# One wait for the four gathers of a half, and the item-0 corrections moved behind the spike counts, in a recurrent spiking recommender on one core

## The chip, the cores and the metric

The kernel runs on one core of a Trainium2 chip. The metric is the time of one execution in microseconds (us) on the device. The prediction was made on 1649.73 us, the median of three runs of the kernel before (1649.36 to 1651.72). All runs of this study were on single cores, but not all on the same chip. That turned out to matter, so each result below says which chip it comes from, by its number. The first pair of measurements, on which the prediction is judged, came without a chip number.

## The reference, cut to what matters

```python
e = emb[seq]                                  # 1024 sequences, 50 items each, rows of 128 floats
prefix = jnp.cumsum(e, axis=1)
denom = jnp.minimum(t_idx[None, :], lengths[:, None])
uF = prefix / denom[:, :, None]
y = (uF - uF.mean(axis=0)) * lax.rsqrt(uF.var(axis=0) + 1e-5) * gamma + beta
# per time step: v += (x - v) / 2; spike = v >= 1; v -= spike
uF_out = spikes.mean(axis=0)
scores = uF_out @ emb.T                       # 1024 x 100001
```

Row 0 of the table counts as zero. The kernel gathers the row as it is and takes it out again with a small matmul; this is the "correction".

## The kernel before

There are two stages. The first goes through the 50 time steps, the second multiplies the spike means by the whole table and stores 409.6 MB of scores. The change is in the first. In each step GpSimd gathers the rows of the next step with eight indirect transfers of 128 rows each. TensorE transposes the eight tiles of this step into two accumulators (`pre[0]`, `pre[1]`, one for each half of the batch). VectorE reads each half (`uF`), takes its statistics, and updates the membrane `v`.

```python
gp = ph.enter_context(tc.tile_pool(name="gather", bufs=2))     # two buffers of e
...
        def gather(t):
            es[t] = gp.tile([P, B], F32, tag="e", name=f"e_{t}")
            for n in range(NB):                                # NB = 8
                nc.gpsimd.indirect_dma_start(
                    out=es[t][:, n * P : (n + 1) * P], out_offset=None, in_=table,
                    in_offset=bass.IndirectOffsetOnAxis(ap=idx[:, n, t : t + 1].bitcast(U32), axis=0),
                )
...
            if t + 1 < T:
                gather(t + 1)
            e = es.pop(t)
            ...
            for h, cs in enumerate(halves):
                for k in range(0, BANK, P):                    # four transposes for each half
                    nc.tensor.matmul(pre[h][:, k : k + P],
                                     lhsT=e[:, h * BANK + k : h * BANK + k + P], rhs=ident,
                                     start=False, stop=last, is_transpose=True, ...)
                nc.vector.scalar_tensor_tensor(uF[:, cs], rlen[:, cs], 1.0 / (t + 1), pre[h], ALU.max, ALU.mult)
                nc.vector.bn_stats(bs[:, h, :], uF[:, cs])
            if not last:
                correct(t + 1, l)                              # two matmuls into pre[0], pre[1]
            ...
            if t and not last:
                nc.vector.tensor_single_scalar(s, v, V_TH, ALU.is_ge)
                counted(t - 1, s)                              # two matmuls into sums[0], sums[1]
            # ... normalisation and the step of v on VectorE and ScalarE
```

## Time and profile before

| | kernel before, first measurement |
|---|---|
| time | 1649.73 us |
| profiled span | 1646.4 us |
| last `uF` of stage 1 starts | 576.37 us |
| last gather starts | 567.84 us |
| a step that nothing holds up | 7.49 us |
| three steps, on average | 33.9 us |
| GpSimd waits "remote" for its buffer | 64.2 us in 16 waits |

In a line of the timeline the first number is the start in us and the second the duration, then come the engine, the line of the source, the operation, output <- inputs, the shape and the number of instructions. The bracket is the idle time of the engine just before, and what ended it. "Remote" means that no instruction in the profile ended just then: what ended the wait was done earlier, and I take it that its semaphore came late: in the stall that the prediction shows, the eight transposes had all started by 308.70 us and were recorded as reported up to 321.10 us. The lines of before that matter stand in the prediction.

### The profile page before, as it was taken

The page shows a single profiled execution, that of the slowest core. Times are in us where ns is not written, and L with a number is a line of the kernel's source. Part 1 is how long each engine was busy: PE and PEld are TensorE (multiplying, and loading weights), DVE is VectorE, ACT ScalarE, POOL GpSimd, SP SyncE. Part 2 cuts the span into 40 slices and gives each one's busy share as a digit, 9 for nine tenths or more (in the row PEclk, how much of TensorE's full clock was granted, in tenths as well). Part 3 has the DMA queues.
Part 4 walks back from the last instruction along what each step waited for, and adds up shares of the span by engine and source line. Part 5 has one row for each costly group of instructions (what it writes and reads, how often), then busy time and mean ns, then how long its engine had stood idle before and what let it go on. Part 6 is the DMA issues. An engine that isn't in the chain of part 4 may idle for free.

```text
span 1646.4 us, 12555 instructions
## 1 busy us (share of the span) xinstructions
PE 1115.2 (68%) x4538; PEld 829.4 (50%) x4548; DVE 940.4 (57%) x1161; ACT 630.6 (38%) x700; POOL 379.3 (23%) x406
## 2 busy tenths in 40 slices
PE   4344433444334498889987888888888888788885
PEld 2122211222113276667766666666666666666664
DVE  4566655666556766557655555555555555555553
ACT  2222222222222255446544444444444444444442
POOL 7666666666666500000000000000000000000000
PEclk9999999999755599999999999999999999999998
DMA  9511111111111179999999999999999999999898
GB/s 342 213 45 48 47 48 43 47 48 48 48 43 49 39 320 412 416 422 398 426 422 429 432 428 427 421 420 429 420 423 412 415 421 421 428 425 423 381 428 350
DMA packets 53691, 488.14 MB, mean 296 GB/s; under 512 B 11995, under 2 KB 12796, under 8 KB 32380
## 3 DMA queue, kind: packets, MB, share of 16 engines
q1 hardware_dynamic: 31984, 428.77, 62.0%
q0 software_dynamic: 12800, 26.24, 5.5%
q10 hardware_dynamic: 8844, 32.33, 5.0%
q8 instruction: 36, 0.59, 0.1%
q14 instruction: 27, 0.22, 0.0%
HBM read 77.69 MB, written 409.60 MB: 296 GB/s over the span
## 4 chain that ended last, share of the span: by engine, by line
DMA 48%; DVE 22%; another core or an unknown queue 10%; PE 9%; ACT 5%; issue 4%; POOL 1%; DVEq 0%; ACTq 0%; SPq 0%
DMA scores<-o 48%; PE po L149 8%; ACT o L456 4%; DVE bs L306 4%; DVE uF L305 4%; DVE v L342 3%; DVE s L326 3%; DVE negv L348 3%; DVE o L454 2%; POOL e L187 1%; DVE a L335 1%; DVE mv L316 1%; DVE q L332 0%; PE pt L119 0%
## 5 line engine op out<-in xcount | busy, mean ns | idle before, releaser
L454 DVE TENSOR_SCALAR o<-po 128x1024 f32<-128x1024 f32 x391 | 463.7, 1221 | 352.4 <-DMA scores<-o 326.9
L456 ACT ACTIVATE o<-po 128x1024 f32<-128x1024 f32 (+1 forms) x391 | 388.0, 1019 | 548.2 <-DMA scores<-o 345.0
L187 POOL DMA_INDIRECT e<-in_L_rec_emb_table,idx x400 | 378.6, 947 | 188.8 <-issue 109.8
L149 PE MATMUL po<-pairs,countB 128*128 128x512 f32 x1168 | 313.9, 415 | 66.8 <-ACT o L456 49.6
L149 PEld LDWEIGHTS po<-pairs,countB 128*128 128x128 f32 x1168 | 225.4, 198 | 131.3 <-ACT o L456 64.4
L149 PE MATMUL po<-pairs,countC 128*128 128x512 f32 x876 | 238.2, 417 | 43.2 <-ACT o L456 43.0
L253 PE MATMUL pre<-zT,l 128*128 128x512 f32 x100 | 74.6, 748 | 247.2 <-DVE uF L305 159.5
L149 PEld LDWEIGHTS po<-pairs,countC 128*128 128x128 f32 x876 | 168.8, 199 | 89.3 <-ACT o L456 54.8
L253 PEld LDWEIGHTS pre<-zT,l 128*128 128x128 f32 x100 | 27.7, 279 | 286.9 <-issue 183.0
L305 DVE SCALAR_TENSOR_TENSOR uF<-rlen,pre 128x512 f32<-128x512 f32 x100 | 68.0, 680 | 180.5 <-remote 145.0
L320 ACT ACTIVATE r<-mv,eps 128x1 f32<-128x1 f32 x50 | 14.7, 295 | 378.8 <-DVE mv L316 269.4
L142 DVE TENSOR_TENSOR pairs<-pt,pairs 128x1024 fp32r<-128x1024 f32 (+1 forms) x73 | 88.4, 1217 | 94.7 <-ACT pairs L141 94.7
L296 PE MATMUL pre<-ident,e 128*128 128x128 f32 x400 | 107.2, 426 | 25.8 <-DMA e<-in_L_rec_emb_table,idx 17.7
L119 PE MATMUL pt<-ident,rows 128*128 128x128 f32 x782 | 113.1, 292 | 8.3 <-ACT o L456 3.7
L119 PEld LDWEIGHTS pt<-ident,rows 128*128 128x128 f32 x782 | 102.3, 154 | 28.6 <-issue 9.8
L296 PEld LDWEIGHTS pre<-ident,e 128*128 128x128 f32 x400 | 85.3, 223 | 60.9 <-DMA e<-in_L_rec_emb_table,idx 32.2
L149 PE MATMUL po<-hi,countB 128*128 128x512 f32 x200 | 82.9, 414 | 19.2 <-ACT o L456 14.9
L264 PE MATMUL sums<-s,ident_h 128*128 128x512 bf16 x88 | 45.3, 606 | 64.2 <-DVE s L326 32.8
L149 PE MATMUL po<-lo,countB 128*128 128x512 f32 x200 | 80.4, 402 | 0.0
L149 PE MATMUL po<-pairs,countA 128*128 128x512 f32 (+1 forms) x292 | 73.5, 393 | 9.1 <-ACT o L456 9.1
L141 ACT CAST pairs<-pt 128x1024 fp32r<-128x1024 f32 (+1 forms) x73 | 73.6, 1008 | 15.0 <-PE pt L119 14.9
L149 PE MATMUL po<-hi,countC 128*128 128x512 f32 x150 | 63.2, 421 | 17.7 <-ACT o L456 17.7
(76 smaller groups left out, 849.8 us busy)
## 6 DMA issues: line engine op xcount, KB each, us to landing
scores<-o SPq DMA_DIRECT2D x96, 3072.0 KB, 20.3
scores<-o SPq DMA_DIRECT2D x32, 1536.0 KB, 9.0
rows<-in_L_rec_emb_table ACTq DMA_DIRECT2D x20, 1536.0 KB, 29.2
scores<-o SPq DMA_DIRECT2D x22, 1024.0 KB, 8.6
rows<-in_L_rec_emb_table SPq DMA_DIRECT2D x6, 3072.0 KB, 42.7
scores<-o SPq DMA_DIRECT2D x8, 2048.0 KB, 13.2
scores<-o SPq DMA_DIRECT2D x8, 1872.5 KB, 11.3
e<-in_L_rec_emb_table,idx POOLq DMA_INDIRECT x400
```

What stands on the lines that cost most here:

```text
L119: nc.tensor.transpose(pt[:, k0 : k0 + kw], r[:kw, k0 : k0 + D], ident[:kw, :kw])
L141: nc.scalar.copy(vh, vp)
L142: nc.vector.tensor_tensor(vl, vp, vh.bitcast(F32), ALU.subtract)
L149: nc.tensor.matmul(po[:, :kw], lhsT=counts[n], rhs=part[:, k0 : k0 + kw], start=j == 0, stop=j == 1,)
L187: nc.gpsimd.indirect_dma_start(out=es[t][:, n * P : (n + 1) * P], out_offset=None, in_=table, in_offset=bass.IndirectOffsetOnAxis(ap=idx[: ...
L253: nc.tensor.matmul(pre[h], lhsT=l, rhs=zT[:, h * BANK : (h + 1) * BANK], start=t == 0, stop=False, skip_group_check=True,)
L296: nc.tensor.matmul(pre[h][:, k : k + P], lhsT=e[:, h * BANK + k : h * BANK + k + P], rhs=ident, start=False, stop=last, is_transpose=True, ...
L305: nc.vector.scalar_tensor_tensor(uF[:, cs], rlen[:, cs], 1.0 / (t + 1), pre[h], ALU.max, ALU.mult)
L306: nc.vector.bn_stats(bs[:, h, :], uF[:, cs])
L326: nc.vector.tensor_single_scalar(s, v, V_TH, ALU.is_ge)
L454: nc.vector.tensor_scalar_mul(o[:, h0 : h0 + hw], po[:, :hw], 1.0 / T)
L456: nc.scalar.mul(o[:, h0 : h0 + hw], po[:, :hw], 1.0 / T)
```

## The change

It is meant to spare waits and semaphore updates on TensorE's queue: the first transpose of a half waits for all four of its gathers, so that the other three need no wait and their increments can be merged; and the corrections come behind the counts, so that they need no wait for VectorE.

```diff
+    def after(ins, other):
+        sync = mybir.DependencyInfo(mybir.DependencyClass.Sync, mybir.DependencyReason.DATA)
+        tc.add_manual_dep(ins.ins, other.ins.name, sync, reason="one wait for several gathers")
...
-                nc.gpsimd.indirect_dma_start(
+                landed[t, n] = nc.gpsimd.indirect_dma_start(
...
-                    nc.tensor.matmul(
+                    turn = nc.tensor.matmul(
...
+                    if k == 0 and not last:
+                        for n in range(1, BANK // P):
+                            after(turn, landed[t, h * BANK // P + n])
...
-            if not last:
-                correct(t + 1, l)
-            else:
+            if last:
...
                 counted(t - 1, s)
+            if not last:
+                correct(t + 1, l)
```

More of the change, by code (lines that the diff above doesn't have):

```diff
@@ L182, in rec_kernel @@
         es = {}
+        landed = {}
         def gather(t):
```

## The prediction

> **What bounds the kernel now.** I read the page first, then the chain of waits in order of time, then the timeline of a few steps of the first stage, and last the semaphore records behind it. The row of slices shows two stages: about 576 us of 50 time steps (GpSimd gathers, DMA almost idle at 45 to 50 GB/s), then 1070 us in which output stores run at some 415 GB/s. The change touches the first stage only, and nothing the second stage waits for except its start: the six big row loads it needs are done in the second of the forty slices. So a microsecond taken from the first stage should be a microsecond of the whole.
>
> ```profile
> POOL 7666666666666500000000000000000000000000
> ...
> DMA  9511111111111179999999999999999999999898
> ...
> L187 POOL DMA_INDIRECT e<-in_L_rec_emb_table,idx x400 | 378.6, 947 | 188.8 <-issue 109.8
> ...
> L305 DVE SCALAR_TENSOR_TENSOR uF<-rlen,pre 128x512 f32<-128x512 f32 x100 | 68.0, 680 | 180.5 <-remote 145.0
> ```
>
> The gathers follow each other every 1.25 us when nothing holds them (947 ns and 0.30 us of issue), so eight cost 10.02 us a step. One undisturbed step takes 7.49 us, and VectorE is busy throughout (7.02 us of records in the 7.48 us from 298.31). Neither explains the stage: v of successive steps starts at 292.25, 299.74, 307.23 and then 326.16 us. Three steps take 33.9 us, 11.3 us each, over the gathers' 10.02. The timeline shows the long one:
>
> ```profile
> 305.79 1.48 PE L296 MATMUL pre<-ident,e 128*128 128x128 f32 x6
> ...
> 307.23 1.23 DVE L342 SCALAR_TENSOR_TENSOR v<-negv,v 128x1024 f32<-128x1024 f32 x1 [0.21 <-DVE negv L348]
> ...
> 307.43 0.47 PE L296 MATMUL pre<-ident,e 128*128 128x128 f32 x1 [0.15 <-issue]
> ...
> 308.70 0.47 PE L296 MATMUL pre<-ident,e 128*128 128x128 f32 x1 [0.80 <-DMA e<-in_L_rec_emb_table,idx]
> ...
> 315.51 0.69 DVE L305 SCALAR_TENSOR_TENSOR uF<-rlen,pre 128x512 f32<-128x512 f32 x1 [7.05 <-remote]
> ...
> 321.12 0.69 DVE L305 SCALAR_TENSOR_TENSOR uF<-rlen,pre 128x512 f32<-128x512 f32 x1 [4.20 <-remote]
> 321.35 0.94 POOL L187 DMA_INDIRECT e<-in_L_rec_emb_table,idx  x1 [4.19 <-remote]
> ```
>
> All eight transposes of the step have started by 308.70 us, the eighth 2.49 us after its gather was issued, so the data is there. Yet uF of the first half, which needs four of them, starts at 315.51, and of the second half at 321.12, 12.4 us after the eighth transpose started. VectorE waits only for TensorE there, so "remote" must be TensorE's completion semaphore arriving late. GpSimd waits for the same eight completions, because e has two buffers, and stands still for 4.19 us. This happens every third step:
>
> ```profile
> DVE uF L305 <- remote: 145.0, 27, 12.4
> ...
> POOL e L187 <- remote: 64.2, 16, 4.4
> ```
>
> The semaphore records say how it is late. Counted back from the two releases, transposes 1 to 5 are reported at 307.78, 310.58, 312.69, 315.48 and 318.28 us, one per 2.1 to 2.8 us; the rest follow quickly (320.38, 320.41, 321.10) once the gathers have stopped at 317.17. In the first step after a stall the reports come at once, 0.21 us apart (291.47, 291.68, 291.89, 292.11). So each report is a queued event that costs 2 to 3 us in the bad stretch. I do not know what makes it slow; it begins after some 11 to 19 us of unbroken gathering and ends when gathering pauses.
>
> [...]
>
> **The change, part by part.** The built programs show what the source does not say.
> 1. Transposes. Before, each of the eight waits for its own gather and raises the semaphore by one. After, the first of a half carries four waits and the other three none, and the increments are merged into one +4 on the fourth. Over the kernel, updates on the transposes fall from 400 to 106. The price is two EventSemaphore instructions per half, 196 in all, 51 ns each in the trace: 0.2 us a step on a queue that is mostly idle.
> 2. Corrections behind the counts. They then need only ScalarE's l, since the counts already waited for a later VectorE instruction. Of 49 EventSemaphore waits one remains, and the updates on corrections and counts fall from 85 + 48 to 45 + 2. A typical step falls from 11 events (8 + 2 + 1) to 3.
> 3. Added latency. The first half's transposes now start only when its fourth gather has landed; four spaced 0.21 us then run where one ran, so each half is ready about 0.65 us later. That shifts every step once and does not lengthen the period. The corrections delay the next transposes by two matmuls: 0.57 + 0.43 us by their spacing at the start of the trace (11.52, 12.09, 12.52). In the undisturbed step the fourth would end near 300.4 instead of 299.4 us and VectorE asks for it at 300.88; the eighth near 301.2, asked for at 302.21. It just fits, at no cost.
> 4. Unchanged: gathers, VectorE and ScalarE work, buffers, the second stage.
>
> What this buys: if the last completion of a step comes less than 8.8 us after its last gather has landed, GpSimd never waits (it asks for the buffer 11.27 us after that gather started, less 2.5 to land). Before it came about 12.4 us late in each stall. With three events, even at 2.8 us each, two of them after the data is there, I estimate 1.1 us + 2 x 2.8 = 6.7 us. GpSimd then runs through: from 3.89 us, 399 intervals of 1.2525 us and the first one's extra 0.2 put the last gather at 503.9 instead of 567.84 us. That is 64 us, the same as its waits in the table above. The two steps that also prepare rows (t = 42 and 44) cost VectorE and TensorE some 5 us each; the 2.5 us a step by which VectorE is quicker than the gathers makes that up by t = 49. The last uF then stands near 508 to 511 instead of 576.4. Full gain: 64 + about 1 = 65 us, to 1585 us.
>
> **The rivals.**
> - The slow reports stay and become the new chain. With gathering unbroken the bad stretch may never end. From one second-half uF to the next the path would be counts and corrections (about 5 us), then three reports of 2.1 to 2.8 us: 11.3 to 13.4 us, over 10.02, until GpSimd stalls again and clears it. For it: the cause of the slowness is not removed. Against: one step in three is slow at worst now with 11 events, and GpSimd has 8 us of slack to eat first. It would give back 15 to 45 us: 1600 to 1630.
> - The inserted waits are the poison. TensorE now sits in EventSemaphore instructions for the gathers of every half while a report is pending, and all data must be there before any transpose. For it: stalls mostly begin where TensorE waits for a gather. Against: at t = 0 and 1 it waited for nearly every gather, and reports came 0.5 us after the transposes; in the stall at 547.92 us no transpose waited. It would be 1650 to 1700.
> - VectorE becomes the bound. At 7.49 us a step it would need 375 us, under the gathers' 501, so only if the added microsecond on TensorE opens a bubble over 2.5 us a step; I see none.
> - The second stage starts earlier into something unready. Its rows are loaded long before; nothing speaks for it.
>
> **Range and chances.** I give some 60% to the full gain (1580 to 1592), 22% to a part of it (1600 to 1630), 12% to about no change and 6% to worse. 2% is 33 us, half of the full gain, so most partial gains count as faster too. I put the time at 1590 us, a little above the full gain, and 1577 to 1635 as the range.
>
> **What would show it.** Right: gathers 1.25 us apart from start to end with GpSimd's "remote" wait near zero instead of 64.2 us; the last gather near 504 us; steps of 10.0 us; the second stage as long as before (1070 us). Step 2 is right if uF starts within 1 to 7 us of its fourth and eighth transpose. Wrong: a "remote" wait of VectorE still over 8 us after the eighth transpose, gathers pausing every few steps, or steps over 11 us; then the number of reports was not what mattered.

## The result

The changed kernel took 1653.82 us (1653.41 to 1654.22, 4 runs), the kernel before 1649.55 us beside it (1647.12 to 1651.72, 4 runs). The ratio is 1.0026, with a 95% interval of 1.0009 to 1.0044: the same within 2%. All ratios here are the mean time of one kernel's fast runs over that of the other's of the same rounds, so they are not quite the ratio of the medians.

First the page of the changed kernel, in the lines that answer to those of before (the busy tenths of GpSimd and DMA in forty slices, then the groups of the gathers and of `uF`: busy us, mean ns, idle us before them with its releaser).

```profile
POOL 6666666666666500000000000000000000000000
...
DMA  9511111111111169999999999999999999999998
...
L192 POOL DMA_INDIRECT e<-in_L_rec_emb_table,idx x400 | 377.6, 944 | 187.2 <-issue 113.4
...
L314 DVE SCALAR_TENSOR_TENSOR uF<-rlen,pre 128x512 f32<-128x512 f32 x100 | 67.9, 679 | 184.3 <-remote 177.4
```

Little has moved. GpSimd's idle time before its gathers is 187.2 us (188.8 before). VectorE's before `uF` is 184.3 us (180.5 before), of which more is put down to late reports, 177.4 us (145.0 before). Now a stall of the changed kernel in its timeline:

```profile
309.51 1.91 PE L301 MATMUL pre<-ident,e 128*128 128x128 f32 x8
...
316.21 0.95 POOL L192 DMA_INDIRECT e<-in_L_rec_emb_table,idx  x1 [0.30 <-issue]
321.17 0.69 DVE L314 SCALAR_TENSOR_TENSOR uF<-rlen,pre 128x512 f32<-128x512 f32 x1 [9.84 <-remote]
321.46 0.94 POOL L192 DMA_INDIRECT e<-in_L_rec_emb_table,idx  x1 [4.30 <-remote]
...
322.50 0.67 DVE L314 SCALAR_TENSOR_TENSOR uF<-rlen,pre 128x512 f32<-128x512 f32 x1
```

All eight transposes run back to back, the fourth starts at 310.15 and the eighth at 311.00 us. Each half is reported by one update. The first half's report comes 11.0 us after its fourth transpose, when gathering has stopped (the last gather ends at 317.16 us), and the second half's comes at once with it (both are recorded, at 321.14 and 321.20 us). So one single report waits as long as four did before. The length of the cycle is unchanged as well: three steps take 33.9 us (from one GpSimd stall to the next, 321.46 to 355.38 us). Within it the second quick step now takes 9.0 us and not 7.49, because the second `uF` waits 1.4 us for a late report (at 305.05 us), and the long step is shorter by as much, 17.5 for 18.9 us.

The second stage is as before: from the last `uF` to the end it is 1651.6 - 581.47 = 1070.1 us, against 1646.4 - 576.37 = 1070.0 us. The 4 us by which the changed kernel is later lie at the end of the first stage. Its last stall falls on step 48 and not on step 47, and its last `uF` starts at 581.47 us instead of 576.37. On chip 8 this offset was absent in one series and 2 us in another (below), so I treat it as a matter of how the cycle of stalls ends; that is not shown.

### The profile page after: what moved, and what is told of

Same layout as the page of the kernel before. It is cut to its first block, busy times and chain, and to the rows that moved or that the text cites. A ratio compares the mean times of both kernels' runs of the same rounds, so it can differ in the third digit from the quotient of the medians.

```text
span 1651.6 us, 12703 instructions
## 1 busy us (share of the span) xinstructions
PE 1077.9 (65%) x4538; PEld 838.0 (51%) x4548; DVE 940.4 (57%) x1161; ACT 631.1 (38%) x700; POOL 378.3 (23%) x406
## 4 chain that ended last, share of the span: by engine, by line
DMA 47%; DVE 23%; another core or an unknown queue 11%; PE 9%; ACT 6%; issue 3%; POOL 0%; DVEq 0%; ACTq 0%; SPq 0%
DMA scores<-o 46%; PE po L149 9%; ACT o L465 4%; DVE bs L315 4%; DVE uF L314 4%; DVE v L351 4%; DVE s L333 3%; DVE negv L357 3%; DVE o L463 2%; DVE a L344 1%; ACT v L348 1%; DVE mv L323 1%; DVE q L340 0%; DVE q L341 0%
## 5 line engine op out<-in xcount | busy, mean ns | idle before, releaser
L192 POOL DMA_INDIRECT e<-in_L_rec_emb_table,idx x400 | 377.6, 944 | 187.2 <-issue 113.4
L149 PE MATMUL po<-pairs,countC 128*128 128x512 f32 x876 | 242.4, 423 | 49.0 <-ACT o L465 48.9
L269 PEld LDWEIGHTS <-ident_h 128*128 128x128 bf16 x98 | 12.3, 125 | 385.3 <-issue 385.3
L314 DVE SCALAR_TENSOR_TENSOR uF<-rlen,pre 128x512 f32<-128x512 f32 x100 | 67.9, 679 | 184.3 <-remote 177.4
L301 PE MATMUL pre<-ident,e 128*128 128x128 f32 x400 | 95.1, 416 | 10.9 <-DMA e<-in_L_rec_emb_table,idx 10.9
L348 ACT ACTIVATE v<-uF,hgb,a 128x1024 f32<-128x1024 f32 x49 | 59.2, 1209 | 37.5 <-issue 18.9
## 6 DMA issues: line engine op xcount, KB each, us to landing
scores<-o SPq DMA_DIRECT2D x8, 1872.5 KB, 11.3
```

Of the source, the lines that this page charges most:

```text
L149: nc.tensor.matmul(po[:, :kw], lhsT=counts[n], rhs=part[:, k0 : k0 + kw], start=j == 0, stop=j == 1,)
L192: landed[t, n] = nc.gpsimd.indirect_dma_start(out=es[t][:, n * P : (n + 1) * P], out_offset=None, in_=table, in_offset=bass.IndirectOffset ...
L301: turn = nc.tensor.matmul(pre[h][:, k : k + P], lhsT=e[:, h * BANK + k : h * BANK + k + P], rhs=ident, start=False, stop=last, is_transpos ...
L348: nc.scalar.activation(vt, uF[:, cs], AF.Identity, bias=hgb[:, 1:2], scale=a)
```

## The experiments

All ask one thing: what holds the reports back. Runs marked "wrong result" were so on purpose. Where several runs have the same kernel they are told together.

### Each part alone, one transpose, and no gathers: chip 4

`waits_only` has the four-gather wait and leaves the corrections in their old place; `order_only` has the corrections behind the counts and no joint waits:

```diff
-                    if k == 0 and not last:
+                    if False:                      # order_only
```

> Part 1 alone: the first transpose of a half waits for four gathers, the corrections stay before the counts. Theory A (a completion of TensorE is held back as long as gathers run, however few there are): same cycle of three steps in about 33.9 us, GpSimd's remote wait 60 to 70 us, time 1648 to 1656 us. Theory B (in the bad stretch each transpose costs 2 to 3 us by itself, and the merged report is simply that of the fourth): the same time, 1648 to 1656 us. The theory on record (the count of reports): below 1600 us. That part 1 lengthens the start or the end by up to 1 us is possible.

> Part 2 alone: corrections behind the counts, each transpose waits for its own gather and reports by itself. Theories A and B: no change of the cycle, 1648 to 1656 us; transposes reported one per 2 to 3 us in the stall, as before. The theory on record: 8 + 2 or 3 reports instead of 11 per step, a small gain, 1630 to 1645 us.

`one_turn` (wrong result) keeps all gathers and waits, and drops three of the four transposes of each half:

```diff
-                for k in range(0, BANK, P):
+                for k in range(0, BANK, P) if t in (0, T - 1) else (0,):
```

> Wrong result on purpose: the changed kernel with one transpose for each half instead of four (steps 1 to 48), all gathers and waits kept. Theory A (held back until gathering pauses): uF still starts 8 to 12 us after the transpose in every third step, GpSimd's remote wait stays 55 us or more, 1640 to 1656 us. Theory B (each transpose takes 2 to 3 us in the bad stretch): uF starts 2 to 6 us after its transpose, GpSimd never or seldom stalls, steps of 10 to 10.4 us, 1583 to 1610 us.

`hw_rows` (wrong result) has plain transfers from SyncE's queue in place of the gathers, to see whether it is the gathers that hold TensorE's reports back:

```diff
-        engine = nc.sync if q < AHEAD * GROUP else nc.scalar
+        engine = nc.scalar
...
-                landed[t, n] = nc.gpsimd.indirect_dma_start(...)
+                c = (t * NB + n) * P
+                landed[t, n] = nc.sync.dma_start(out=es[t][:, n * P : (n + 1) * P], in_=table[c : c + P, :])
```

> Wrong result on purpose: the changed kernel with each gather replaced by a plain transfer of 128 consecutive rows from SyncE's queue (the six large row loads go to ScalarE's queue); same bytes, same buffers, same waits of TensorE. [...]no wait of VectorE for a transpose that has been issued for over 2 us, steps bound by VectorE at 7.5 to 8.5 us once the row loads are through, the first stage below 450 us. If it is the DMA traffic and its semaphore writes as such, or TensorE waiting for four transfers: waits of 5 us or more stay.

| chip 4 | median us | ratio to before | 95% interval |
|---|---|---|---|
| before (31 runs) | 1576.26 | | |
| waits_only (12 runs) | 1576.86 | 1.0004 | 0.9996 to 1.0013 |
| order_only (12 runs) | 1576.47 | 1.0001 | 0.9992 to 1.0010 |
| one_turn (12 runs, wrong result) | 1577.70 | 1.0009 | 1.0000 to 1.0018 |
| hw_rows (1 run, wrong result) | 1500.58 | | |

The surprise is in the first row. The kernel before, unaltered, took 1576.26 us here and 1649.55 us there. All 31 runs lie between 1575.97 and 1576.93, so this is no state that comes and goes. None of the theories about reports could be tested, because on this chip none is late: in the profiles of the first three GpSimd has no "remote" wait at all. Their gathers run 1.25 us apart from first to last and bound the stage. `hw_rows` shows what lies under that bound: without the gathers a step takes 7.48 us, and the last `uF` starts at 429.50 us.

### The same two kernels again: chips 0, 8 and 3

The question was now whether the chip makes the stall. The changed kernel was sent again four times unaltered, and the kernel before once for its profile. The chip could not be chosen.

> The changed kernel itself, unaltered, because the kernel before took 1576 us on the chip of the last four runs and 1650 us where the prediction was measured. Theory C (the long reports belong to the chip or its condition, not to the number of reports): on a chip where before takes 1576 us, 1576 to 1579 us, all uF within 2 us of the transpose, gathers 1.25 us apart throughout, ratio 0.998 to 1.002; on one where before takes 1650 us, 1652 to 1655 us with the cycle of three steps. The theory on record (the count of reports sets the stall) would have after well below before wherever before stalls.

> The kernel before, unaltered, for its profile on the same chip. Theory C: its time goes with the profile: at 1576 us no remote wait of GpSimd over 2 us in the first stage, last gather at 503 to 505 us, all 11 reports of a step within 2 us of their instruction; at 1650 us the cycle of 33.9 us with reports 2 to 3 us apart. A low granted clock (0.5) in the first stage may occur in either; if it went with the stall it would only be seen beside 1650 us.

> The changed kernel unaltered once more, to have it beside the kernel before on a chip that does not stall, if this is one: 1576 to 1578 us against 1576, ratio 1.000 to 1.001 (each part alone gave 1.0004 and 1.0001). If the chip stalls: ratio 1.001 to 1.003 as on the first two.

> The changed kernel unaltered, for a chip on which before takes 1576 us: 1576 to 1578 us, ratio 1.000 to 1.001, since the gathers at 1.25 us each bound the first stage there and the change leaves them as they are. If the chip stalls: ratio 1.000 to 1.003.

> The changed kernel unaltered. On a chip where before takes 1576 us: 1576 to 1578 us, ratio 1.000 to 1.001. Where before takes about 1650 us: ratio 1.000 to 1.003, nothing new.

| run | chip | before, median us | changed, median us | ratio | 95% interval |
|---|---|---|---|---|---|
| after_again | 0 | 1652.53 (15 runs) | 1653.88 (12) | 1.0013 | 1.0002 to 1.0023 |
| after_again_2 | 8 | 1649.29 (23) | 1648.62 (20) | 1.0000 | 0.9990 to 1.0010 |
| after_again_3 | 8 | 1652.70 (15) | 1654.57 (12) | 1.0007 | 0.9997 to 1.0018 |
| after_again_4 | 3 | 1577.33 (15) | 1577.82 (12) | 1.0003 | 0.9995 to 1.0012 |

`before_again`, on chip 0, took 1648.91 us in its one run, and its profile has the stalls of the first one (GpSimd "remote" 64.5 us in 16 waits, against 64.2). So there are chips on which both kernels stall and chips on which neither does: chips 0, 8 and 13 (below) at about 1650 us, chips 3, 4 and 11 at about 1577 us. Chip 8 was met twice and stalled both times, the others once each. Which core of the chip ran is not on record, so "chip" here means all that came with that number. On neither kind does the change do anything. For the kernel before, the medians on chips 0 and 4 (1652.53 and 1576.26 us) have a ratio of 1.048. Nearly all of it lies in the first stage: from the last `uF` to the end the changed kernel takes 1576.1 - 507.38 = 1068.7 us on chip 3, and the two first profiles have 1070.0 and 1070.1 us.

This is the changed kernel on chip 3. The first lines are of its page (GpSimd, granted TensorE clock and DMA by slices), then come two lines of its waits (total us, times, longest):

```profile
POOL 6777777777776000000000000000000000000000
PEclk9865555555555999999999999999999999999998
DMA  9611222222121999999999999999999999999998
```

```profile
POOL e L192 <- issue: 115.9, 380, 0.3
DVE uF L314 <- PE pre L301: 110.0, 47, 3.1
```

GpSimd is done about one slice earlier (a slice is 39 to 41 us). It has little but its 0.30 us between gathers, and VectorE waits at most 3.1 us for a `uF`, now for TensorE's own work on data that has just come. The timeline of a step:

```profile
301.74 1.05 PE L301 MATMUL pre<-ident,e 128*128 128x128 f32 x4
...
303.46 0.68 DVE L314 SCALAR_TENSOR_TENSOR uF<-rlen,pre 128x512 f32<-128x512 f32 x1
...
306.00 0.94 POOL L192 DMA_INDIRECT e<-in_L_rec_emb_table,idx  x1 [0.30 <-issue]
...
306.19 1.09 PE L301 MATMUL pre<-ident,e 128*128 128x128 f32 x4 [3.40 <-DMA e<-in_L_rec_emb_table,idx]
...
307.32 0.69 DVE L314 SCALAR_TENSOR_TENSOR uF<-rlen,pre 128x512 f32<-128x512 f32 x1 [2.45 <-PE pre L301]
```

The fourth transpose of the second half starts at 306.86 us, and `uF` follows 0.46 us later, with gathers running all the time. The granted clock is no cause: this profile has 0.5 in most of the first stage and does not stall, the first profile of before has 0.9 in most of it and stalls:

```profile
PEclk9999999999755599999999999999999999999998
```

The semaphore records of the traces differ too. Between 100 and 500 us the trace of chip 3 holds 640 increments on each of the eight gather semaphores, for 320 gathers: 640 x 8 / 320 = 16 for each gather. The trace of the same kernel on chip 0 holds 78 to 220, where 282 gathers of 16 would give 564. In the stall that the prediction shows, TensorE's own reports are recorded 2.1 to 2.8 us apart, and the last of them 0.7 us after the one before (320.41 to 321.10 us), which are multiples of some 0.7 us.

### Repeats that met a chip without stalls: chip 11

`one_turn_2` and `hw_rows_2` are the same kernels as above, and `paced` sets a small memset of GpSimd behind each gather:

```diff
+                nc.gpsimd.memset(pause, 0.0)          # 128 x 8
```

> The same kernel as one_turn (one transpose for each half, wrong result on purpose), because the chip of the first call showed no stall in any kernel. Only where before takes about 1650 us does it tell anything. Theory A (a report is held until gathering pauses): uF 8 to 12 us after its transpose in every third step, 1640 to 1656 us. Theory B (in the bad stretch each instruction of TensorE, or each unit of the semaphore, takes 2 to 3 us): uF of the first half 2 to 6 us after its transpose, a step of six instructions at 2 to 3 us is 12 to 17 us against 24 to 34, stalls rarer, 1590 to 1630 us. Where before takes 1576 us: 1577 us.

> The same kernel as hw_rows (plain transfers of the same size from SyncE's queue in place of the gathers, wrong result on purpose). Where before takes about 1650 us: if GpSimd's gathers hold the reports back, no wait of VectorE for TensorE over 3 us after the row loads, steps of 7.5 us, about 1500 us as on the other chip. If the chip is slow with any such traffic, or TensorE's reports are slow by themselves: waits of 5 us or more and over 1550 us. Where before takes 1576 us: 1500 us.

> The changed kernel with a small memset (128x8) by GpSimd behind every gather, so that gathers come at an even, lower rate. If the stall comes from a backlog that builds up while GpSimd gathers without a gap (it begins 11 to 19 us after a restart), a slower even rate, up to 1.40 us a gather, takes it away: no remote wait of GpSimd, steps of 8 times the new period, 1590 to 1640 us where before takes 1650. If only a real pause helps: stalls as before plus the memsets' time in the gathering, 1655 to 1700 us. Where before takes 1576 us: 400 times the memset's time more, 1600 to 1660 us.

Before took 1575.99 us, so none of the three tells anything of the stall: 1577.40, 1501.65 and 1580.89 us. The memset (125 ns) vanished almost wholly in the 0.30 us between gathers, so that gathers came every 1.26 us on average. It was too small to be of use.

### Six kernels in one: chip 13

Because the chip could not be chosen, I cut the fifty steps into parts with one experiment in each, so that one look on a chip that stalls would answer them all.

```diff
+            if 30 <= t < 42:                          # plain transfers: 8 a step, from 36 on 1 a step
+                w = NB if t >= 36 else 1
+                ... nc.sync.dma_start(...)
+                return
...
+                if 17 <= t < 30:                      # slower gathers
+                    nc.gpsimd.memset(countB[:, : 160 if t < 24 else 400].bitcast(F32), 0.0)
...
-                for k in range(0, BANK, P):
+                for k in (0,) if 9 <= t < 17 else range(0, BANK, P):
```

> Wrong result on purpose; the changed kernel with its fifty steps cut into parts, so that one look on a chip that stalls answers several questions. Steps 2 to 8: unaltered. 9 to 16: one transpose for each half. 17 to 23: a memset of 128x160 by GpSimd behind each gather (a gather every 1.36 us or so). 24 to 29: a memset of 128x400 (every 1.5 us). 30 to 35: plain transfers from SyncE's queue, eight a step. 36 to 41: one plain transfer a step. 42 to 49: unaltered. On a chip where before takes 1576 us: no wait of VectorE for TensorE that outlasts the data by 2 us anywhere; it tells nothing else. On one where before takes 1650 us. Theory A (held until gathering pauses): lags of 8 to 12 us also with one transpose, none with plain transfers. Theory B (2 to 3 us an instruction or unit of TensorE): with one transpose lags of 2 to 6 us. Theory D (every semaphore event, above all the 16 of each transfer, goes through a path that on this chip is too slow): stalls also with eight plain transfers a step, which bring 128 events in 7.5 us, but none with one a step (16 events); the slower pace of gathers (1.36 or 1.5 us) makes the stalls rarer or ends them. Theory E [...]: no stalls in either part with plain transfers.

It met chip 13, where before took 1649.81 us in one run; this kernel took 1605.32 us. A step is counted from the start of one second-half `uF` to the next in the trace. Each part is compared with the unaltered part of the same execution. A wait of up to some 2 us in the last column need be no late report: VectorE may be busy with its own work then.

| steps | what | gather interval us | us a step | longest wait from the last transpose to `uF`, us |
|---|---|---|---|---|
| 3 to 8 | unaltered | 1.25 | 11.13 | 12.2 |
| 9 to 16 | one transpose for each half | 1.25 | 11.18 | 10.6 |
| 17 to 23 | memset of 160 columns | 1.36 | 11.32 | 8.3 |
| 26 to 29 | memset of 400 columns | 1.56 | 12.49 | 0.5 |
| 31 to 35 | eight plain transfers | none | 7.48 | 1.7 |
| 37 to 41 | one plain transfer | none | 7.54 | 1.9 |

Four things follow. First, with a quarter of the transposes, which raise the semaphore by a quarter as much, the step still takes 11.2 us. This fells theory B (each instruction costs 2 to 3 us) and, once more, the theory on record. Second, theory D falls: eight plain transfers in 7.48 us bring more semaphore events each microsecond than the gathers (128 in 7.48 us, against 128 in 10.0 us for eight gathers at 1.25 us), all of them are in the trace (80 or 96 on each of their eight semaphores in 45 us, five or six times 16), and nothing stalls (lines below). That left theory E (the stall comes with the transfers that GpSimd issues, and not with SyncE's), which the next section narrows to indirect gathers. Third, the slower gathers at 1.56 us do not stall, though GpSimd works without a pause. So unbroken gathering as such (theory A) is not it either. Fourth, every part that stalls takes the same 11.1 to 11.3 us a step. Eight gathers in 11.3 us are 1.41 us a gather, the number that 33.9 us for 24 gathers gives as well.

```profile
362.58 1.91 PE L314 MATMUL pre<-ident,e 128*128 128x128 f32 x8
...
364.33 0.68 DVE L327 SCALAR_TENSOR_TENSOR uF<-rlen,pre 128x512 f32<-128x512 f32 x1
364.52 3.65 SPq L195 DMA_DIRECT2D e<-in_L_rec_emb_table  x8
...
365.66 0.67 DVE L327 SCALAR_TENSOR_TENSOR uF<-rlen,pre 128x512 f32<-128x512 f32 x1
```

These are the eight plain transfers: all eight transposes have run by 364.49 us, and both `uF` follow without a wait.

The part with one transpose shows also that the slow reports are not TensorE's alone:

```profile
167.07 1.17 DVE L346 TENSOR_SCALAR s<-v 128x1024 bf16<-128x1024 f32 x1
...
170.47 1.01 PE L282 MATMUL sums<-s,ident_h 128*128 128x512 bf16 x2 [12.00 <-remote]
...
172.54 0.16 DVE L353 TENSOR_TENSOR q<-r 128x1 f32<-128x1 f32 x1 [3.70 <-remote]
...
173.93 0.16 DVE L354 SCALAR_TENSOR_TENSOR q<-mv,q 128x1 f32<-128x1 f32 x1 [1.24 <-issue]
...
174.65 0.15 DVE L355 TENSOR_SCALAR q<-q 128x1 f32<-128x1 f32 x1 [0.56 <-DVE q L354]
...
176.05 0.27 DVE L357 TENSOR_SCALAR a<-q,r,hgb 128x1 f32<-128x1 f32 x1 [1.25 <-DVE q L355]
```

VectorE's `s` is done at 168.24 us, and TensorE, which waits only for it, starts at 170.47. The four tiny instructions of VectorE, each of which waits for the one before, start 1.39, 0.72 and 1.40 us apart. In the profile of chip 3 the same chain starts 0.20, 0.19 and 0.19 us apart (from 300.13 us). So while the stretch lasts, VectorE's reports pass slowly too, in steps of about 0.7 us. In the ordinary stalls lateness shows on TensorE alone; I take it that this is because the other engines stand still then and have little to report, which is not shown.

### The rate at which it begins, and what it goes with: chip 8

Theory F now said: on such a chip the path that the gathers load, and that the reports share, takes about 1.41 us a gather. GpSimd puts one in each 1.25 us, the backlog grows, reports wait in it, GpSimd then stands still for want of a buffer, and the backlog drains. `rates` (wrong result) tests that with finer steps, and splits gathers in half:

```diff
+            cols = 268 if 2 <= t < 13 else 220 if 21 <= t < 32 else 0
...
+                for u in (slice(0, P // 2), slice(P // 2, P)) if 13 <= t < 21 else (slice(0, P),):
+                    landed[t, n] = nc.gpsimd.indirect_dma_start(out=es[t][u, ...], ...)
+                if cols:
+                    nc.gpsimd.memset(countB[:, :cols].bitcast(F32), 0.0)
```

> Wrong result on purpose (in steps 13 to 20 the second 64 rows of a gather use the first 64 indices). It tells something only where before takes about 1650 us. Theory F: on such a chip the path that GpSimd's gathers load, and that TensorE's reports share, takes about 1.41 us a gather of 128 rows (24 gathers in 33.9 us); GpSimd puts in one each 1.25 us until it is full, and reports wait until it has drained; so a step can't be under 11.3 us however the reports are arranged. Steps 2 to 12, a memset of 128x268 behind each gather, about one each 1.45 us: no stall, all reports within 2 us, steps of 11.6 us. Steps 21 to 31, 128x220, about 1.41 us: at the edge, few short stalls, steps of 11.3 us. Steps 33 to 41, unpaced: stalls, and 11.3 us a step on average. Steps 13 to 20, each gather split into two of 64 rows: if the load goes with rows, 11.3 us a step or GpSimd's own time if that is longer, and then no stalls; if it goes with the number of transfers (and their semaphore writes), 16 times 1.41 = 22.6 us a step with stalls. Were it not a rate at all but the mere presence of unbroken gathering, 1.45 us would stall as 1.25 us does.

`rates_2` (wrong result) halves the rows of a gather without doubling the number of gathers, looks once more at the edge, and lets GpSimd itself issue plain transfers (the large row loads go to ScalarE's queue here, as in `hw_rows`):

```diff
+                if 24 <= t < 35:
+                    landed[t, n] = nc.gpsimd.dma_start(out=es[t][:, n * P : (n + 1) * P], in_=table[c : c + P, :])
+                    continue
+                u = P // 2 if 2 <= t < 13 else P
+                if u < P:
+                    nc.sync.dma_start(out=es[t][u:, n * P : (n + 1) * P], in_=table[c + u : c + P, :])
...
+                if 13 <= t < 24:
+                    nc.gpsimd.memset(countB[:, :190].bitcast(F32), 0.0)
```

> Wrong result on purpose. It tells something only where before takes about 1650 us. Steps 2 to 12: each gather takes 64 rows only, and a plain transfer from SyncE's queue brings 64 others; GpSimd issues one each 1.21 us. If the limit goes with GpSimd's transfers: stalls, and 1.41 to 1.47 us a gather, 11.3 to 11.8 us a step. If it goes with rows: no stalls, 9.7 us a step. Steps 13 to 23: whole gathers with a memset of 128x190 behind each, one each 1.38 us: the limit lies between 1.36 (stalls) and 1.41 us (none); either no stall and 11.05 us a step, or rare stalls and 11.3. Steps 24 to 34: plain transfers of 128 rows from GpSimd's own queue. If any transfer that GpSimd makes loads the path: stalls as in the unaltered steps, unless GpSimd takes over 1.4 us for one; if only the indirect ones: none.

Both met chip 8, where before took 1649.29 us (23 runs) and 1652.70 us (15 runs). `rates` took 1744.66 us and `rates_2` 1636.19 us, one run each.

| steps | what | GpSimd's interval us | us a step | stalls |
|---|---|---|---|---|
| rates, 7 to 12 | memset of 268 columns | 1.45 | 11.61 | none |
| rates, 24 to 31 | memset of 220 columns | 1.41 | 11.29 | none |
| rates, 33 to 41 | unaltered | 1.25 | 11.67 | three, of up to 12.5 us |
| rates, 13 to 20 | 16 gathers of 64 rows | 1.21 | 23.55 | waits of up to 25.9 us |
| rates_2, 3 to 12 | 8 gathers of 64 rows, 8 plain ones | 1.21 | 11.66 | one every second step |
| rates_2, 13 to 23 | memset of 190 columns | 1.39 | 11.09 | one, in steps 20 and 21 |
| rates_2, 24 to 34 | 8 plain transfers by GpSimd | 0.53 | 7.48 | none |

A step at an even 1.41 us in the timeline of `rates`:

```profile
431.03 1.09 PE L305 MATMUL pre<-ident,e 128*128 128x128 f32 x4
431.19 0.95 POOL L194 DMA_INDIRECT e<-in_L_rec_emb_table,idx  x1 [0.17 <-issue]
...
432.14 0.29 POOL L201 MEMSET countB<- 128x220 f32 x1
432.60 0.95 POOL L194 DMA_INDIRECT e<-in_L_rec_emb_table,idx  x1 [0.17 <-issue]
432.74 0.68 DVE L318 SCALAR_TENSOR_TENSOR uF<-rlen,pre 128x512 f32<-128x512 f32 x1
```

VectorE goes from `v` (431.60 us, 1.23 us long) straight to `uF`, so it does not wait for the transposes, and GpSimd never stops. In the same execution reports came 10 to 26 us late in the parts at 1.21 us (before this one) and at 1.25 us (after it). So the stall is a matter of rate: none at 1.41 us and slower, one in eleven steps at 1.39, and the full stalls at 1.36 (chip 13), 1.25 and 1.21.

The halved gathers tell what the rate counts. Sixteen of 64 rows took 23.55 us a step, which is 1.47 us each. Eight of 64 rows took 11.66 us, 1.46 us each. Half of the rows is no relief, so the limit goes with the number of gathers. A stall in the part with sixteen gathers, where the four transposes from 232.21 us are reported 26 us later, when GpSimd has stood still for 9 us:

```profile
232.21 1.09 PE L305 MATMUL pre<-ident,e 128*128 128x128 f32 x4 [0.78 <-DMA e<-in_L_rec_emb_table,idx]
...
248.97 0.90 POOL L194 DMA_INDIRECT e<-in_L_rec_emb_table,idx  x1 [0.30 <-issue]
...
258.80 0.69 DVE L318 SCALAR_TENSOR_TENSOR uF<-rlen,pre 128x512 f32<-128x512 f32 x1 [9.08 <-remote]
259.04 0.90 POOL L194 DMA_INDIRECT e<-in_L_rec_emb_table,idx  x1 [9.16 <-remote]
```

And of the transfers tried it goes with the gathers alone: GpSimd's own plain transfers of the same size do not meet it.

```profile
345.60 0.68 DVE L323 SCALAR_TENSOR_TENSOR uF<-rlen,pre 128x512 f32<-128x512 f32 x1
345.99 4.22 POOL L194 DMA_DIRECT2D e<-in_L_rec_emb_table  x8 [0.74 <-PE pre L310]
...
346.93 0.67 DVE L323 SCALAR_TENSOR_TENSOR uF<-rlen,pre 128x512 f32<-128x512 f32 x1
...
353.09 0.68 DVE L323 SCALAR_TENSOR_TENSOR uF<-rlen,pre 128x512 f32<-128x512 f32 x1
```

Eight are issued in 4.22 us, and the steps are 7.49 us apart (353.09 - 345.60), which is VectorE's own time.

No version in this study beats the two kernels with a right result. On a chip that stalls the first stage needs, by an estimate from the measured 1.41 us, 400 x 1.41 = 564 us for its gathers whatever the reports do, and pacing them at 1.41 us would only make the same time even. On the others they need, by the same estimate, 400 x 1.25 = 500 us (on chip 3 the last one starts at 503.65 us).

## Why the prediction was wrong

**The bound.** The prediction read correctly that neither the gathers at GpSimd's own pace (10.02 us a step) nor VectorE (7.49 us) explains 11.3 us, and that the late reports hold VectorE and GpSimd up. It did not ask why the average was so steady. Three steps of 33.9 us are 1.41 us a gather, and the 64.2 us that GpSimd waited are 400 gathers times the 0.16 us between 1.41 and 1.2525. Both numbers stood in the text. They suggest that something behind GpSimd takes gathers at that rate, and that the waits are how it is enforced. The parts with slower gathers agree (no stall at 1.41 us and slower); what it is that takes them was not shown.

**The step that failed** is "With three events, even at 2.8 us each, two of them after the data is there, I estimate 1.1 us + 2 x 2.8 = 6.7 us", and with it "GpSimd then runs through". It takes the 2 to 3 us as the price of one report. The stall of the changed kernel shows one report that took 11.0 us, and the part with one transpose shows late reports of VectorE too. The runs fit, without showing it, a report that is slow because it shares a path that gathers have filled: its wait would end when they have drained, and fewer reports would not drain them. An earlier sentence, "it begins after some 11 to 19 us of unbroken gathering and ends when gathering pauses", would describe a backlog that fills and empties. I said that I did not know its cause and built the estimate on its symptom. The signs that the prediction named for being wrong all came: a `uF` 11.5 us after the eighth transpose, gathers that pause in every third step, and 11.3 us a step.

How the reports share the path is not shown. A queue in which each waits its turn does not fit. At 310.15 us 19 gathers had been issued since the restart at 287.52 us; by an estimate from 1.41 and 1.25 us the backlog was 19 x 0.16 = 3 us, and yet the report took 11.0 us. What fits is a report that comes through only when the gathers have drained, by the same estimate 24 x 0.16 = 3.8 us after the last of them; it came 4.0 us after (317.16 to 321.14 us). But in the kernel before some reports did come through meanwhile, 2.1 to 2.8 us apart.

**What held.** The counting of instructions and updates was right, and so was the claim that the corrections and the joined waits cost nothing: undisturbed steps of the changed kernel take 7.49 us, and where nothing stalls the whole change costs nothing clear of noise (1577.82 against 1577.33 us). The arithmetic of a stage without stalls was right to a few us. It put the last gather at 503.9 us, the last `uF` at 508 to 511 and the end at 1585. On chip 3 these are 503.65, 507.38 and 1577.8 us, the end 7 us lower. But the kernel before has that time there too: it is not the change that brings it. The second stage did stay as long as it was.

**The rivals.** The first, "The slow reports stay", named the right ground ("the cause of the slowness is not removed"), but it still gave back 15 to 45 us, because it too thought of a chain of reports. No shorter chain gains anything while the gathers set 11.3 us a step. The second, that the inserted waits are harmful, has nothing for it: `waits_only` is at 1.0004 where nothing stalls, and the whole change is at 1.0000 to 1.0026 where it does. The third and fourth did not occur.

**What is shown and what is open.** Shown: the stall depends on the chip; on the two such chips where that was tried (8 and 13, each part in one execution) it comes from indirect gathers closer than about 1.4 us (full stalls at 1.36 us and less, one in eleven steps at 1.39, none at 1.41 and more) and holds back the reports of TensorE and, in one part, of VectorE; on chip 8 it goes with their number and not with their rows. Open: which path that is, and why only some chips have it. Every run of this study was recorded in the same way, and the records of semaphores themselves thin out in the stall, and at an even 1.41 us already without one (367 of some 848 in the 75 us from 380 us of `rates`). The count of records alone is not the load: GpSimd's plain transfers on chip 8 left 16.7 semaphore records of their own each us (320 to 385 us of `rates_2`), none missing, where gathers every 1.25 us would leave 12.8. But whether recording is part of the load can't be told from these runs.

## What to carry to other kernels

When a stall repeats with a steady period, divide the period by each kind of work in it before you explain the waits. Here 33.9 us for 24 gathers was 1.41 us a gather with either arrangement of the waits; it behaved as a rate limit, and rearranging what waits behind it gained nothing (ratios of 1.0000 to 1.0026). A change that is to save an engine's waits is first to be tried on a second chip with the kernel before, since a wait that only some chips have is no property of the kernel alone: here one kernel took about 1577 us on chips 3, 4 and 11 and about 1650 us on chips 0, 8 and 13. Where the chip can't be chosen, put several experiments into parts of one run: its unaltered part is then the control.
